# Fourier stage of a four-layer hybrid network: the order of the filler steps inside each slot

## The chip, the core and the metric

The kernel runs on one core of one Trainium2 chip, as one launch. The metric is the device time of a run in microseconds; the median of three runs of the kernel before is 4054.6 us.

## What is computed

The network has four layers on a tensor of 4 images, 96 channels and 64 x 64 pixels, all in float32: a state-space layer, a convolution block, an attention layer with a quantised feed-forward, and a Fourier mixing layer with another quantised feed-forward. The change touches the Fourier mixing alone. Its input is the token sequence `t` (4 batches of 4096 tokens of 96 channels), normalised over the channels:

```
def _ln_t(v, eps=1e-5):
    m = jnp.mean(v, axis=-1, keepdims=True)
    s = jnp.var(v, axis=-1, keepdims=True)
    return (v - m) / jnp.sqrt(s + eps)

h = jnp.einsum('bnc,hc->bnh', x, w1)
h = jax.nn.relu(_bn(h, bn1_gamma, bn1_beta, bn1_mean, bn1_var))
X = jnp.fft.fft(h, axis=1, norm='ortho')
rd = jnp.diagonal(r)
idg = jnp.diagonal(i)
xr = jax.nn.relu(X.real * rd - X.imag * idg + rb)
xi = jax.nn.relu(X.imag * rd + X.real * idg + ib)
y = jnp.fft.ifft(xr + 1j * xi, axis=1, norm='ortho').real.astype(jnp.float32)
o = jnp.einsum('bnh,ch->bnc', y, w2)
return _bn(o, bn2_gamma, bn2_beta, bn2_mean, bn2_var)

t = t + fourier(_ln_t(t))
```

The hidden width is 192, and the transform runs over the 4096 tokens.

## The kernel before

**Units and slots.** `fourier` (line 1083) cuts the work into 8 units, a unit being one batch and one half (96) of the hidden channels. A unit holds 24 groups of 4 channels and is worked on in 4 portions of 6 groups (`PER` = 4), so there are 32 portions, `its`. A loop over slots `j` (line 1259) is a software pipeline over them: slot j begins portion j and does later steps of earlier portions. The 4096-point transform is split into 128 x 32 points.

**The main steps of a slot**, in their order:

- `over_n1(j)` (line 1141): six products with `dft1` on PE (L1147) into `s1`, two multiplications by twiddle factors on DVE (L1151) into `p0` and `p1`, two additions on POOL (L1159) into `f`.
- `fold(j - 2)` (line 1189): a ReLU on ACT over half of `av` (L1193), four DVE operations (L1198, L1201) that add or subtract pairs into `zz` and `z64`, and a negation on ACT (L1204).
- `over_k1` of a first block (line 1233): part of the inverse transform of a unit two units back. It loads a table `gt` (L1235, on SP), runs four products (L1238), and copies the result to `ys` on ACT (L1240).
- `over_n2(j - 1)` (line 1161): four products with `dft2` (L1168 to L1171) into `xi` and `xr`, one DVE multiplication (L1174) into `ec`, twelve ACT operations (L1183) into `av`, and two additions on POOL (L1186, L1187).
- `w2` of the first block (line 1242, product L1246, addition to `t` on DVE at L1250 or L1252), then `over_k1` of a second block.
- `over_k2(j - 3)` (line 1206): twelve products (L1216, L1217) and two ACT copies to `bt` (L1218).
- `w2` of the second block.

Blocks of the inverse transform exist in slots 8 to 39, portions to begin in slots 0 to 31.

**The filler steps** prepare the next batch:

- `norm1` (line 1101) is the centring of 512 tokens: a product with a matrix of ones (L1104), the subtraction of the mean on DVE into `h` (L1105), the square on ACT into `ln_sq` (L1107). 
- `norm2` (line 1109) is the sum of squares of the same tokens: a product with ones (L1111), Ln and Exp on ACT into `ln_rs`, which has one buffer (L1113, L1114), and the multiplication of `h` on POOL (L1115). 
- `w1` (line 1126) is a token product: two products (L1133) and two ReLU evictions on ACT (L1135) into `hh`, for two of the 32 token columns at a time. It needs all of the batch's `h`.
- `row64` (line 1223) closes a unit's forward transform: a product (L1226), an ACT copy to `r64` (L1228), a DMA to DRAM (L1230) and a DMA from there into row 64 of `bt` (L1231). The first `over_k1` of that unit reads `bt`.

Slots 0 to 3, 8 to 11 and 16 to 19 hold norm steps (called norm slots here), 16 steps per batch; slots 4 to 7, 12 to 15 and 20 to 23 hold four token products each (token slots); `row64` falls in slots 7, 11, 15, 19, 23, 27, 31 and 35. Apart from row64, slots 24 to 31 have no filler.

**What sets the order.** The body runs under `tc.manual_schedule` for PE, DVE, ACT and POOL, so each of these engines issues its instructions in the order in which the Python code calls the steps. Before, the slot collects its main steps in a list `main` and its filler steps in a list `fill`, and spreads the filler evenly behind the main steps:

```
left = len(main)
for f0 in main:
    f0()
    take = -(-len(fill) // left)
    for f1 in fill[:take]:
        f1()
    fill, left = fill[take:], left - 1
```

SP, which issues the DMAs, is not in that set; its order comes from the scheduler.

**The ring of two banks.** `norm1`, `norm2`, `w1`, `row64`, `over_k1` and `w2` all take their result tile from `misc` (line 1097), a pool of two PSUM banks (`m_ps` in the profile). So each of these products waits until the product two before it in this ring has been read by its DVE or ACT reader. `s1`, `xi`, `xr` have one bank group each, `i1` two.

Of the kernel before, what the change touches and what calls it, by code (L numbers as in the profile page):

```python
# [18 lines left out]
B, C, HW, L = 4, 96, 64, 4096  # L19
# [3 lines left out]
MB = 512  # L23
# [27 lines left out]
class Net:  # L51
# [1031 lines left out]
    def fourier(self, dram, t, h):  # L1083
        tc, nc, ins = self.tc, self.nc, self.ins
        CG, G, K1 = 24, 6, 65
        PER = CG // G
        units = [(b, half) for b in range(B) for half in range(2)]
        its = [(u, g) for u in range(len(units)) for g in range(0, CG, G)]
        with ExitStack() as ctx:
# [11 lines left out]
            def norm1(b, a, kept):  # L1101
                ps = misc(C)
                x = t[:, b * L + a : b * L + a + MB]
                nc.tensor.matmul(ps, self.ones, x, start=True, stop=True)  # L1104
                nc.vector.scalar_tensor_tensor(h[:C, a : a + MB], ps, -1.0 / C, x, ALU.mult, ALU.add)  # L1105
                kept[a] = wk.tile([C, MB], F32, name="ln_sq", tag="sq", bufs=2)
                nc.scalar.activation(kept[a], h[:C, a : a + MB], AF.Square)  # L1107

            def norm2(a, kept):
                ps = misc(C)  # L1110
                nc.tensor.matmul(ps, self.ones, kept.pop(a), start=True, stop=True)  # L1111
                rs = wk.tile([C, MB], F32, name="ln_rs", tag="rs")
                nc.scalar.activation(rs, ps, AF.Ln, scale=1.0 / C, bias=self.eps[:C])  # L1113
                nc.scalar.activation(rs, rs, AF.Exp, scale=-0.5)  # L1114
                nc.gpsimd.tensor_mul(h[:C, a : a + MB], h[:C, a : a + MB], rs)  # L1115

            def norm(b):
                kept = {}
                steps = [lambda a=a: norm1(b, a, kept) for a in range(0, L, MB)]
                steps2 = [lambda a=a: norm2(a, kept) for a in range(0, L, MB)]  # L1120
                order = steps[:1]
                for one, two in zip(steps[1:], steps2):
                    order += [one, two]
                return order + steps2[-1:]

            def w1(b, n):

                if n == 0:
# [12 lines left out]
            def over_n1(i):  # L1141

                u, g = its[i]
                ps = pln.tile([128, 2, MB], F32, name="s1_ps", tag="s1")
                for d in range(G):
                    a = d % 3 * 2 * K1
                    nc.tensor.matmul(ps[:, d // 3, a : a + 2 * K1], hh[u][:, g + d], self.dft1, start=True, stop=True)  # L1147
                pp = []
                for k in range(2):
                    p = wk.tile([128, G, 2, K1], F32, name=f"p{k}", tag=f"p{k}")  # L1150
                    nc.vector.tensor_mul(  # L1151
                        p.rearrange("p (a g) r k -> p a g (r k)", a=2),
                        ps[:, :, : 6 * K1].rearrange("p a (g k) -> p a g k", g=3),
                        self.twid[:, k : k + 1, None, :].to_broadcast([128, 2, 3, 2 * K1]),
                    )
                    pp.append(p)
                f[i] = wk.tile([128, 2, G, K1], F32, name="f", tag="f", bufs=2)
                for r in range(2):
                    nc.gpsimd.tensor_add(f[i][:, r], pp[0][:, :, r, :], pp[1][:, :, 1 - r, :])  # L1159
# [29 lines left out]
            def fold(i):  # L1189

                u, g = its[i]
                v = av.pop(i)
                nc.scalar.activation(v[:, 1:3], v[:, 1:3], AF.Relu)  # L1193
                z = zz[i] = wk.tile([128, G, 3, K1 - 1], F32, name="zz", tag="zz", bufs=2)
                if g == 0:
                    z64[u] = wk.tile([128, 2, CG], F32, name="z64", tag="z64", bufs=2)
                for k, (one, two, op) in enumerate(((0, 2, ALU.add), (3, 1, ALU.subtract))):
                    nc.vector.scalar_tensor_tensor(  # L1198
                        z[:, :, 1 + k], v[:, one, :, : K1 - 1], 0.0, v[:, two, :, : K1 - 1], ALU.max, op
                    )  # L1200
                    nc.vector.scalar_tensor_tensor(  # L1201
                        z64[u][:, k, g : g + G], v[:, one, :, K1 - 1], 0.0, v[:, two, :, K1 - 1], ALU.max, op
                    )
                nc.scalar.mul(z[:, :, 0], z[:, :, 2], -1.0)  # L1204
# [18 lines left out]
            def row64(u):  # L1223
                ps = misc(CG)[:, :128]
                for k in range(2):
                    nc.tensor.matmul(ps, z64[u][:, k], self.dft64[:, k], start=k == 0, stop=k == 1)  # L1226
                r = wk.tile([CG, N2, 4], F32, name="r64", tag="r64", bufs=2)
                nc.scalar.copy(r, ps.rearrange("p (n c) -> p n c", c=4))  # L1228
                d = dram.tile([1, N2 * C], F32, name="d64", tag="d64", bufs=2)
                nc.sync.dma_start(d.rearrange("o (n g c) -> g (o n) c", n=N2, c=4), r)  # L1230
                nc.sync.dma_start(bt[u][64:65].rearrange("p n c -> p (n c)"), d)  # L1231

            def over_k1(u, n, kept):
                gt = wk.tile([N1, 4, N1], F32, name="gt", tag="gt", bufs=2)
                nc.sync.dma_start(gt, ins["idft"][:, n : n + 4])  # L1235
                ps = misc(C).rearrange("p (n a) -> p n a", n=4)
                for d in range(4):
                    nc.tensor.matmul(ps[:, d], bt[u][:, n + d], gt[:, d], start=True, stop=True)  # L1238
                kept[u, n] = wk.tile([C, MB], F32, name="ys", tag="ys", bufs=2)
                nc.scalar.copy(kept[u, n], ps.rearrange("p n a -> p (n a)"))  # L1240

            def w2(u, n, kept):

                b, half = units[u]
                ps = misc(C)
                nc.tensor.matmul(ps, self.a_w2[:, half, :], kept.pop((u, n)), start=True, stop=True)  # L1246
                ps = ps.rearrange("p (n a) -> p n a", n=4)
                td = ft[b][:, n : n + 4]
                if half == 0:
                    nc.vector.scalar_tensor_tensor(td, ps, self.b2, td, ALU.add, ALU.add)  # L1250
                else:
                    nc.vector.tensor_add(td, td, ps)  # L1252

            engines = {mybir.EngineType.PE, mybir.EngineType.DVE, mybir.EngineType.Activation, mybir.EngineType.Pool}
            with tc.manual_schedule(engines=engines):
                for n in range(0, N2, 2):
                    w1(0, n)
                kept = {}
                for j in range(len(its) + 12):
                    main, fill = [], []  # L1260
                    ub, k = divmod(j - 2 * PER, PER)
                    if j < len(its):
                        main.append(lambda j=j: over_n1(j))
                    blocks = [(ub, n) for n in (8 * k, 8 * k + 4)] if 0 <= ub < len(units) else []
                    if 2 <= j < len(its) + 2:
                        main.append(lambda j=j: fold(j - 2))
                    if blocks:
                        main.append(lambda: over_k1(*blocks[0], kept))
                    if 1 <= j < len(its) + 1:
                        main.append(lambda j=j: over_n2(j - 1))  # L1270
                    if blocks:
                        main.append(lambda: (w2(*blocks[0], kept), over_k1(*blocks[1], kept)))
                    if 3 <= j < len(its) + 3:
                        main.append(lambda j=j: over_k2(j - 3))
                    if blocks:
                        main.append(lambda: w2(*blocks[1], kept))

                    u, k = divmod(j, PER)
                    if (j - 7) % PER == 0 and 0 <= (j - 7) // PER < len(units):
                        fill.append(lambda j=j: row64((j - 7) // PER))  # L1280
                    if u + 2 < len(units):
                        b = u // 2 + 1
                        if u % 2 == 0:
                            steps = norm(b) if k == 0 else steps
                            fill += steps[4 * k : 4 * k + 4]
                        else:
                            fill += [lambda b=b, n=n: w1(b, n) for n in range(8 * k, 8 * k + 8, 2)]
                    left = len(main)
                    for f0 in main:
                        f0()  # L1290
                        take = -(-len(fill) // left)
                        for f1 in fill[:take]:
                            f1()
                        fill, left = fill[take:], left - 1


def build(tc, ins, out):
# [155 lines left out]
```

## Time and profile before

| What | us |
|---|---|
| runs: lowest, median, highest | 4048.9, 4054.6, 4059.6 |
| the profiled execution's own time | 4057.1 |
| its span, first to last instruction | 4054.9 |
| Fourier stage in the span, from the first token product to the next stage | 3316 to 3911 |
| slots 0 to 3, one by one | 7.8, 7.9, 9.1, 17.4 |
| slots 4 to 7, one by one | 20.8, 10.2, 10.4, 14.1 |
| slots 8 to 11, one by one | 20.4, 20.7, 20.6, 20.5 |
| slots 12 to 15, one by one | 18.7, 20.2, 20.2, 18.8 |
| slots 16 to 23 | as 8 to 15, within 0.3 |
| slots 24 to 31 | 11.6 each |

The length of a slot is the time from its first L1147 product to that of the next slot, read from the timeline of PE. Over the whole span PE is busy 82%, DVE 79%, POOL 73% and ACT 60%; most of it lies in other stages. The view of windows gives busy times for chosen stretches; the chain of waits follows the work that ended last backwards, so a line in it is something that delayed the end; in the timeline a bracket at the end of a line gives the idle time before it and what ended it.

### The profile page before, as it was taken

To read this page: it belongs to the slowest core of one execution; us is meant where nothing else is said; L and a number is where in the kernel's file an instruction comes from. 1 tells how busy PE (TensorE), PEld (TensorE's weight loads), DVE (VectorE), ACT (ScalarE), POOL (GpSimd) and SP (SyncE) were. 2 spreads that over 40 slices of the span, in tenths; PEclk is the share of its full clock that TensorE was granted. 3 is DMA by queue.
4 is the path that set the end of the run, shared out by engine and by line. 5 is a ranking of instruction groups with operands and counts; after the bars stand their busy time and mean duration, and the time that the engine had idled before them with its cause. 6 is when DMAs were issued, how large, how long until landed. Compare 5 with 4: busy or idle time off the path is not lost. (4 is left out here: it accounts for less than half of the span.)

```text
span 4054.9 us, 45522 instructions
## 1 busy us (share of the span) xinstructions
PE 3311.5 (82%) x14174; PEld 1426.9 (35%) x14174; DVE 3193.0 (79%) x2772; ACT 2423.0 (60%) x4644; POOL 2946.8 (73%) x1571
## 2 busy tenths in 40 slices
PE   6888888888888777888888887678999887887987
PEld 3222222222222222222222221376446345556642
DVE  5999999999999999999999999724632763443649
ACT  4666667666667666666766665322445665544547
POOL 2999999999999999999999999511010455333428
PEclk8788878888878888887888887668999998889989
DMA  7667567666756666675675666363000000001111
GB/s 182 144 158 172 136 150 169 158 148 163 175 130 167 168 148 160 158 171 135 162 173 141 160 165 159 103 189 136 0 1 1 1 6 3 27 27 30 45 43 54
DMA packets 183291, 468.13 MB, mean 115 GB/s; under 512 B 53236, under 2 KB 55166, under 8 KB 179968
## 3 DMA queue, kind: packets, MB, share of 16 engines
q1 hardware_dynamic: 183048, 465.21, 46.1%
q8 instruction: 113, 1.85, 0.2%
q14 instruction: 130, 1.06, 0.1%
HBM read 391.53 MB, written 73.50 MB: 115 GB/s over the span
## 5 line engine op out<-in xcount | busy, mean ns | idle before, releaser
L496 POOL TENSOR_TENSOR hs<-hs,crep 128x1024 f32<-128x1024 f32 x768 | 1797.1, 2363 | 28.8 <-DVE hs L490 24.0
L454 PE MATMUL rep<-dbl,sel_b 32*128 32x512 f32 x1152 | 403.8, 777 | 467.8 <-DVE hs L490 441.3
L474 POOL TENSOR_TENSOR up<-udb,brep 128x1024 f32<-128x1024 f32 x256 | 604.5, 2361 | 8.5 <-DMA brep<-cd 8.5
L468 ACT ACTIVATE da<-ddb,nega 128x1024 f32<-128x1024 f32 x512 | 584.8, 1149 | 13.5 <-DVE hs L490 6.9
L468 ACT ACTIVATE dap<-ddb,nega 128x1024 f32<-128x1024 f32 x256 | 286.3, 1118 | 419.9 <-DVE hs L490 417.9
L515 PE MATMUL y<-hs,sel_r 128*32 128x512 f32 x3072 | 477.9, 693 | 4.9 <-POOL hs L496 4.9
L490 DVE TENSOR_TENSOR_SCAN hs<-da,state,rep 128x1024 f32<-128x1024 f32 x192 | 450.9, 2348 | 16.7
L490 DVE TENSOR_TENSOR_SCAN hs<-da,state,u 128x1024 f32<-128x1024 f32 x192 | 450.9, 2348 | 11.2 <-DVE u L486 1.4
L490 DVE TENSOR_TENSOR_SCAN hs<-dap,state,up 128x1024 f32<-128x1024 f32 x192 | 447.2, 2329 | 6.4 <-ACT dap L468 6.0
L210 PE MATMUL ps<-n,w_x 97*64 97x512 f32 x1536 | 376.1, 633 | 6.9 <-ACT n L323 5.4
L454 PEld LDWEIGHTS rep<-dbl,sel_b 32*128 32x128 f32 x1152 | 108.4, 216 | 766.9 <-issue 519.3
L486 DVE TENSOR_TENSOR u<-udb,rep 128x1024 f32<-128x1024 f32 x256 | 314.7, 1229 | 46.2 <-PE rep L454 15.0
L486 DVE TENSOR_TENSOR rep<-udb,rep 128x1024 f32<-128x1024 f32 x256 | 310.8, 1214 | 0.3
L1038 POOL CAST hq<-y 128x512 fp8e5<-128x512 f16 x192 | 117.7, 638 | 222.3 <-issue 136.6
L210 PEld LDWEIGHTS ps<-n,w_x 97*64 97x64 f32 x1536 | 110.6, 143 | 261.5 <-issue 215.7
L1186 POOL TENSOR_TENSOR av<-av,ec 128x780 f32<-128x780 f32 x32 | 58.8, 1837 | 197.2 <-ACT av L1183 191.8
L515 PEld LDWEIGHTS y<-hs,sel_r 128*32 128x32 f32 x3072 | 65.7, 116 | 358.0 <-issue 190.0
L382 POOL TENSOR_TENSOR du<-delta,xc 128x512 f32<-128x512 f32 x96 | 122.8, 1279 | 66.0 <-DMA gp_x<-in_x 51.2
L224 PE MATMUL ps<-xc,xproj 64*102 64x512 f32 x384 | 160.9, 1001 | 3.5 <-ACT xc L344 3.5
L911 POOL MEMSET h<- 1x4096 f32 x1 | 3.5, 3506 | 212.4 <-DVE n L824 212.4
L358 ACT COPY dbl<-ps 102x512 f32<-102x512 f32 x64 | 34.4, 589 | 205.7 <-PE ps L224 205.7
L490 DVE TENSOR_TENSOR_SCAN hs<-da,rep 128x1024 f32<-128x1024 f32 x64 | 146.5, 2289 | 5.4
(256 smaller groups left out, 6573.1 us busy)
## 6 DMA issues: line engine op xcount, KB each, us to landing
ddb<-dd SPq DMA_DIRECT2D x768, 128.0 KB, 3.6
udb<-ud SPq DMA_DIRECT2D x768, 128.0 KB, 4.4
crep<-cd SPq DMA_DIRECT2D x512, 128.0 KB, 4.3
brep<-cd SPq DMA_DIRECT2D x256, 128.0 KB, 3.4
dd<-delta SPq DMA_DIRECT2D x64, 384.0 KB, 4.9
ud<-du SPq DMA_DIRECT2D x192, 128.0 KB, 2.4
band<-in_band SPq DMA_DIRECT2D x24, 1024.0 KB, 5.8
gt<-in_idft SPq DMA_DIRECT2D x64, 256.0 KB, 2.8
```

What stands on the lines that cost most here:

```text
L210: nc.tensor.matmul(ps[rows], w[:, 64 * p : 64 * p + 64], rhs[:, at.start + shift : at.stop + shift], start=k == 0, stop=k == len(ws) - 1, ...
L224: nc.tensor.matmul(ps, w[rows, p], x[rows, p], start=start and p == 0, stop=p == 2)
L382: nc.gpsimd.tensor_mul(u, m["delta"][:, of], m["xc"][:, of])
L454: nc.tensor.matmul(x[:, at], sel_b[rows, order[t][1]], made[k]["dbl"][rows, at], start=True, stop=True)
L468: nc.scalar.activation(da, made[k]["dd", h, j], AF.Exp, scale=nega[:, col : col + 1])
L474: nc.gpsimd.tensor_mul(u, made[k]["ud", h, j], made[k]["brep", g])
L486: nc.vector.tensor_mul(u, made[k]["ud", h, j], x)
L490: nc.vector.tensor_tensor_scan(hs[:, 1:], made[k].pop(("da", t)), u, 0.0 if s == 0 else st, ALU.mult, ALU.add)
L496: nc.gpsimd.tensor_mul(hs[:, :T], hs[:, 1:], made[k]["crep", order[t][1]])
L515: nc.tensor.matmul(made[k]["y", p][row : row + 32], sel_r, made[k]["hs", t][:, at], start=False, stop=True, skip_group_check=True,)
L1038: nc.gpsimd.tensor_copy(q[:, m, :], y2, saturate=False)
L1186: nc.gpsimd.tensor_add(v[:, 2:4], v[:, 0:2], ec)
```

## The change

The even spreading is gone. The function `norm`, which made the list of norm steps, is removed, and the loop calls each step in an order written out by hand. The steps, their instructions, their tiles and buffers, and the slot in which each main step stands are the same. In a norm slot k = 0 to 3 of a batch, `norm1` of block 2k comes before the fold, `norm2` of the block before it after the first `over_k1`, `norm1` of block 2k + 1 after `over_n2`, and `norm2` of block 2k after `over_k2`; the last `norm2` of the batch ends slot k = 3. In a token slot, two token products come before the fold and two after `over_k2`; in the first token slot (k = 0) the first two come after the second `over_k1` instead. `row64`, which before came directly after `over_n1`, comes after `over_k2`, ahead of the last token products and the last `w2`.

```
-            def norm(b):
...
-                return order + steps2[-1:]
...
-                kept = {}
+                kept, sq = {}, {}
                 for j in range(len(its) + 12):
...
+                    def turn(count):
+                        for _ in range(min(count, len(tokens))):
+                            w1(b, tokens.pop(0))
+
                     if j < len(its):
+                        over_n1(j)
+
+                    if normed:
+                        norm1(b, a, sq)
+                    if k:
+                        turn(2)
                     if 2 <= j < len(its) + 2:
+                        fold(j - 2)
                     if blocks:
+                        over_k1(*blocks[0], kept)
+                    if normed and k:
+                        norm2(a - MB, sq)
                     if 1 <= j < len(its) + 1:
+                        over_n2(j - 1)
+                    if normed:
+                        norm1(b, a + MB, sq)
                     if blocks:
+                        w2(*blocks[0], kept)
+                        over_k1(*blocks[1], kept)
+                    if not k:
+                        turn(2)
                     if 3 <= j < len(its) + 3:
+                        over_k2(j - 3)
+                    if normed:
+                        norm2(a, sq)
+                    if (j - 7) % PER == 0 and 0 <= (j - 7) // PER < len(units):
+                        row64((j - 7) // PER)
+                    turn(len(tokens))
                     if blocks:
+                        w2(*blocks[1], kept)
+                    if normed and k == PER - 1:
+                        norm2(a + MB, sq)
```

Here `a` is the first token of block 2k, `b` the next batch, `normed` is true in the norm slots, and `tokens` holds the four token products of a token slot.

## The prediction on record

> **What bounds the kernel now.** The change lies in the Fourier stage, 3316 to 3911 us, so the page's 79 to 82% shares, ruled by layer 0, say little. I read the windows of that stage first. The rows shown are cut where the kind of filler changes, by the start of each slot's first over_n1 product: slots 0 to 7 (norm, then tokens, without the inverse transform), 8 to 11 (norm), 12 to 15 (tokens), 24 to 31 (no filler). 16 to 23 repeat 8 to 15. Columns: window, length, busy time and instructions of PE, PEld, DVE, ACT and POOL, clock, DMA.
>
> ```profile
> core 0: us, PE busy (x) PEld busy (x) DVE busy (x) ACT busy (x) POOL busy (x), PEclk, DMA share, GB/s
> 3333.45:3431.14 97.69, 78.10 (x372) 57.87 (x373) 37.60 (x55) 59.03 (x164) 48.68 (x37) 0.91 0.01 1
> 3431.14:3513.39 82.25, 67.80 (x292) 42.33 (x293) 34.72 (x43) 40.05 (x94) 34.32 (x25) 0.86 0.09 27
> 3513.39:3594.00 80.61, 64.08 (x341) 50.48 (x339) 31.26 (x38) 37.85 (x109) 24.59 (x17) 0.96 0.10 27
> 3751.79:3844.42 92.63, 84.26 (x522) 63.64 (x521) 61.82 (x72) 53.72 (x146) 47.07 (x31) 1.00 0.17 47
> ```
>
> Four norm slots take 82.2 us and four token slots 80.6, while eight slots without filler take 92.6, or 11.6 each. Filler costs 9 us a slot, though its PE work is 4 products of 0.86 = 3.4 us (norm) or 8 of 0.46 = 3.7 us (tokens), from start to start in the timeline. In the norm slots the clock is 0.86. No engine is full: the stage runs on waits. The chain of waits between 3450 and 3480 us shows one whole period.
>
> ```profile
> 3453.03 0.87 PE m_ps L1111 x2
> ...
> 3454.70 0.63 ACT ln_rs L1114
> 3455.34 0.75 ACT av L1193
> ...
> 3457.31 1.22 DVE z L1201
> 3458.53 0.47 DVE zz L1198
> 3459.00 0.08 DVE z L1201
> 3459.08 0.61 DVE h L1105
> 3459.69 0.04 issue
> 3459.73 2.02 PE m_ps L1111 x2
> 3461.75 1.30 PE xi_ps L1168 x2
> ```
>
> A sum of squares (L1111) heads the slot; its Ln and Exp hold ACT until 3455.3; only then comes the fold's ReLU (L1193), then the fold on DVE, then the subtraction (L1105) that frees one of the two m banks, and only then may PE run the next sum of squares and, behind it in order, over_n2. PE idles 3.89 us there and then runs slowly. The waits of PE on the token side have the same shape:
>
> ```profile
> 3535.29 1.04 PE L1238 MATMUL m_ps<-gt,bt 128*96 128x128 f32 x8
> 3539.44 1.35 PE L1133 MATMUL m_ps<-a_w,h 97*128 97x192 f32 x4 [3.11 <-ACT hh L1135]
> ```
>
> The second token product's eviction stands behind the fold's negation on ACT, and the fourth user of the bank waits for it.
>
> **What the skill says.** The Trainium skill, TensorE: Matmul & The Clock Gate, Part 1: idle time drops the array to half its clock for about a window of activity. The trace agrees: xi_ps takes 1.30 to its successor after the 3.89 us wait, 0.65 in a plain slot, where gaps of 1.2 us leave the clock at 1.00. Same page, Architectural detail: ACT, DVE and POOL are strict first-in-first-out; agrees, since ready evictions wait behind the fold. SBUF — State Buffer, Two separate sides: a DVE operation with two SBUF inputs and a GpSimd one exclude each other; agrees: the fold's four operations take 2.9 us beside L1159 and 1.1 us alone. DMA: Bandwidth & Descriptors, Rules for kernel authors: issue a DMA early and wait late; the change does the opposite for row64, costed below.
>
> **Part by part.** No instruction is added or removed; the order of the two built programs does differ as the diff says on PE, DVE, ACT, POOL and SP. Times t count from the slot's first over_n1 product. I walk each engine's new order by hand with durations of the trace.
>
> *Norm slot with blocks (9, 10, 17, 18).* PE: over_n1 to 1.34, centring product to 2.2. DVE: twiddles 1.6 to 3.4, subtraction to 4.05. PE: over_k1 to 3.15, waits 0.95 for the subtraction's bank, sum of squares 4.1 to 4.95, over_n2 (4 x 0.65) to 7.6. ACT: square to 4.65, ReLU to 5.5; the fold no longer meets L1159 (3.5 to 5.35), so 1.1 us, to 6.6; negation 7.1, ys 7.6, Ln and Exp 8.75, twelve av to 12.3. PE: second centring waits for ys's bank to 7.7, ends 8.55; w2 9.4; over_k1 10.35; over_k2 (2.68) 13.0; sum of squares 13.9; w2 14.75. ACT then has square, ys, two bt, Ln and Exp and ends at 15.4, before the next square at 18.8. POOL has the first multiply by ln_rs (L1115, 1.26) at 8.85 to 10.1, the av pair to 16.1 and the second multiply to 17.35, before the next ReLU (19.4) and twiddle sum (18.2); ln_rs has one buffer, so each Ln waits for the multiply before it, 10.1 here and 14.2 when it is wanted. Now 20.7, then 14.75: **-6.0 x 4 = -23.8**. The new wait, ReLU behind the square, costs the ReLU about 1 us against now, and is paid for by the missing Ln and Exp. Slots 8 and 16 lack one sum of squares (13.85), but meet row64 (below): 20.5 to 14.3, **-12.3** for two. Slots 11 and 19 have a third sum of squares, row64 and waits of w2 and of that sum for their banks; its Ln waits for POOL's av pair and multiply and runs 2 us into the next slot, hidden by that slot's row64 wait: 20.5 to 16.5, **-8**.
>
> *Token slot (13, 14, 21, 22).* PE: over_n1 1.34, two token products 3.15, over_k1 4.1 (its bank's evictions are first on ACT, 2.9), over_n2 6.7. ACT: evictions to 3.75, ReLU 4.55; fold beside L1159 until 5.4, to 6.5; negation, ys 7.35; av to 10.9. w2 waits for ys, 7.5 to 8.4; over_k1 9.3; over_k2 12.0; two token products 13.8; w2 14.65. Now 20.2: **-5.55 x 4 = -22.2**. Slots 15 and 23 add row64 and a token product that waits for its copy: 18.8 to 15.7, **-6.2**.
>
> *Slots 0 to 7.* Same walk: slots 0 to 3 41.4 against 42.2 (POOL's av pair, 3.7, and two Ln/Exp pairs still end slot 3); slot 4 14.0 against 20.8, since over_n2 now covers most of the 8.82 us that the first token product waits for POOL; 5 and 6 stay at 10.3; slot 7 12.6 against 14.1. **-9**.
>
> *row64, moved from the slot's head to its end.* Its copy starts two DMAs on SP that the next unit's first over_k1 needs.
>
> ```profile
> 3876.40 0.33 SPq L1230 DMA_DIRECT2D d<-r x1
> 3878.02 0.33 SPq L1235 DMA_DIRECT2D gt<-in_idft x1
> 3880.51 0.24 SPq L1231 DMA_DIRECT2D bt<-d x1
> ```
>
> Issue to issue is 2.9 to 4.4 us over the eight, and PE starts 2.1 us after the last second issue (3882.61): 5.1 to 6.5 us from copy to product. Now over 10 us of work covers it (3788.6 to 3799.4 in slot 27) except once, at the tail. SP is in order, but in the new program the next unit's first two gt loads stand ahead of d, and the eight behind bt aren't due for a slot, so no load is late. Cover left after the copy: row64's followers plus over_n1, 4.35 (slots 8, 16), 2.3 (12, 20), 3.7 (24), 1.85 (28), 0.45 (32). The uncovered rest, less 1.2 us that w2's wait for ys gives back, with 5.8 for the pair: slots 8, 16 inside the numbers above; 12, 20: 3.5 - 1.1 = +2.4, which with a clean walk of 16.4 (the first two token products there wait for w2's addition to 8.4 and for the second ys to 10.15) makes 18.8 against 18.75, **0**; 24 +1, 28 +2.7, 32 +4.1, tail (36, later by w2 and over_k1) +2: **+9.8**. A PE wait of that length lets the clock drop; after 2.2 to 3.9 us it cost 1.75 to 2.75 us in the norm slots (row of L1111 to w2, 6.1 and 7.1 against 4.34 warm); 2 x 4 boundaries (12, 20, 28, 32) = **+8**.
>
> *Sum.* -23.8 - 12.3 - 8 - 22.2 - 6.2 - 9 + 9.8 + 8 = -63.7. The profiled execution took 4057.1 (span 4054.9 and 2.2 around it), so 3993.4; it lies 2.5 above the median 4054.6 of the three, so **3991**. Unknown ends: fold beside POOL 1.1 or 2.9 (8 norm slots: 0 to +14); DMA pair 5.1 to 6.5 (-5 to +5); clock drops at none or all eight boundaries (-8 to +14); handshakes of the walk, -0.2 to +0.5 a slot over 16 (-3 to +8).
>
> **Rivals.** *Row chain hidden.* If fold and ACT catch up during the wait, the +9.8 + 8 and the two +2.4 vanish: 3991 - 23 = 3968. For: DVE and ACT are 42 to 49% busy there. Against: plain slots have only 1.2 us of PE idle. *New order binds elsewhere.* The square ahead of the ReLU makes the fold the chain again, 1.8 us in eight norm slots, and the clock drops once in each of 16 slots (1.0 on average): -64 becomes -34, 4021. For: ReLU is the start of every chain today. Against: the walk leaves it 3 us. *Slower.* The row chain dominates: place, the eight unit boundaries; the clean gain is 64 + 9.8 + 8 + 4.8 = 87 us, so it turns when a boundary costs over 87/8 = 10.9 us, and ends at 4071 at 13 us each (10 us of wait and 3 of cold clock). For: SP is in order and holds bt until d has landed. Against: the pair is 6.5 at most today. *No change*: order arrives but the waits move whole, 4055; the plain slots, 11.6 on the same queues, speak against it.
>
> **Numbers.** Forecast 0.58, hidden 0.16, binds elsewhere 0.17, no change 0.05, slower 0.04. 0.3% (12 us) is about what a measurement of this kernel can tell. Faster 0.91, same 0.05, slower 0.04. Range 3960 to 4022: it takes in the hidden case, the one that binds elsewhere and most of the sum of the unknown ends, and leaves the last two out.
>
> **What would show it.** Right: norm slots of 14.5 to 15.5 us and token slots near 15; L1105 no longer releasing L1111 for 3.89 us; clock above 0.93 between slots 8 and 23; the first over_k1 of a unit waiting on a DMA for 1 to 5 us. Wrong: slots still near 20 with another releaser of PE, or DMA waits over 8 us at each boundary.

## The result and the profile after

The changed kernel took 4006.5 us (median of four runs, 4002.6 to 4009.9) against 4054.1 for the kernel before beside it: ratio 0.9876, 95% interval 0.9864 to 0.9888. In a later measurement beside the kernel before (run after_again below) it was 4003.6 against 4053.0, ratio 0.9877, 0.9861 to 0.9892. The forecast was 3991, the range 3960 to 4022.

Two profiled executions of the changed kernel are used, one of 4009.9 us ("after") and one of 4000.7 ("after_again"). From the first token product to the next stage's first product the Fourier stage took 597.1 us before, 544.5 in the first and 537.1 in the second: 52.6 and 60.0 less. Code lines below over_n1 are 9 lower than before (over_n1 is L1138, `over_k1` L1229).

The windows of the profile after, cut like those of before: slots 0 to 7, 8 to 11, 12 to 15 and 24 to 31.

```profile
core 0: us, PE busy (x) PEld busy (x) DVE busy (x) ACT busy (x) POOL busy (x), PEclk, DMA share, GB/s
3335.96:3431.80 95.84, 80.79 (x373) 59.31 (x373) 40.70 (x55) 59.12 (x164) 50.38 (x38) 0.92 0.01 1
3431.80:3493.90 62.10, 59.25 (x293) 38.67 (x294) 30.05 (x44) 39.82 (x96) 31.28 (x24) 0.96 0.11 35
3493.90:3561.00 67.10, 60.26 (x325) 49.32 (x324) 27.93 (x36) 36.95 (x107) 24.99 (x18) 0.95 0.12 33
3687.82:3792.79 104.97, 85.77 (x522) 64.95 (x520) 64.36 (x77) 55.45 (x148) 48.94 (x32) 0.98 0.15 41
```

Four norm slots went from 82.2 to 62.1 us and four token slots from 78.0 (3513.39 to 3591.35; the window shown with the prediction reached 2.6 us into slot 16) to 67.1; PE is busy nearly all of a norm slot now, and the granted clock (PEclk) rose from 0.86 to 0.96. Slots 0 to 7 hardly moved (97.7 to 95.8), and the eight slots without filler became **longer**, 92.6 to 105.0 (slot 31 here runs to the first `over_k1` of slot 32, so that product's wait is in it). The chain of waits after shows slot 9, the period that headed the prediction:

```profile
3447.45 1.35 PE s_ps L1138 x12
3448.88 1.84 DVE p L1142 x2
3450.73 0.61 DVE h L1105
3451.38 1.10 PE m_ps L1111 x2
3452.48 0.66 PE xi_ps L1159 x2
...
3455.10 0.95 PE m_ps L1104 x2
3456.05 0.86 PE m_ps L1237 x2
3456.91 1.03 PE m_ps L1229 x8
...
3460.62 0.86 PE m_ps L1111 x2
3461.49 0.86 PE m_ps L1237 x2
3462.34 1.35 PE s_ps L1138 x12
```

The fold, its ReLU and Ln and Exp are gone from the chain. The subtraction (L1105) stands right behind the twiddles; from there on PE runs from product to product, `xi_ps` at 0.66 instead of 1.30. The waits of PE in the stage show what went and what came (columns: total, times, longest). Before:

```profile
PE m_ps L1111 <- DVE h L1105: 20.8, 7, 3.9
```

After:

```profile
PE m_ps L1229 <- DMA bt<-d: 16.6, 5, 5.6
...
PE m_ps L1229 <- issue: 8.3, 2, 4.8
PE m_ps L1111 <- DVE h L1105: 6.9, 7, 1.8
```

L1105 held PE for 20.8 us before and holds it for 6.9 now, at most 1.8. New are waits of a unit's first `over_k1` for row 64; the two put down to "issue" are of the same kind. The start of slot 12, on PE and on SP:

```profile
3498.73 1.99 PE L1229 MATMUL m_ps<-gt,bt 128*96 128x128 f32 x8 [3.33 <-DMA bt<-d]
3500.51 1.49 PE L1159 MATMUL xi_ps<-f,dft 128*128 128x390 f32 x2
```

```profile
3492.88 0.33 SPq L1221 DMA_DIRECT2D d<-r  x1
3496.05 0.24 SPq L1222 DMA_DIRECT2D bt<-d  x1
```

Row64's copy ends near 3492.9, the second DMA is issued 3.2 us later, and PE gets its data another 2.7 us later: 5.9 us, of which PE's other work covers 2.5. The eight products then take 1.99 us instead of 1.04.

### The profile page after: what moved, and what is told of

It is laid out like the page before. It is cut to its first block, busy times and chain, and to the rows that moved or that the text cites. A ratio compares the mean times of both kernels' runs of the same rounds, so it can differ in the third digit from the quotient of the medians.

```text
span 4007.8 us, 45514 instructions
## 1 busy us (share of the span) xinstructions
PE 3303.4 (82%) x14174; PEld 1425.1 (36%) x14174; DVE 3186.9 (80%) x2772; ACT 2421.0 (60%) x4644; POOL 2944.4 (73%) x1571
## 5 line engine op out<-in xcount | busy, mean ns | idle before, releaser
L468 ACT ACTIVATE da<-ddb,nega 128x1024 f32<-128x1024 f32 x512 | 584.9, 1149 | 14.9 <-DMA ddb<-dd 7.4
L210 PE MATMUL ps<-n,w_x 97*64 97x512 f32 x1536 | 368.0, 622 | 8.1 <-ACT n L323 5.4
L486 DVE TENSOR_TENSOR u<-udb,rep 128x1024 f32<-128x1024 f32 x256 | 314.6, 1229 | 42.1 <-PE rep L454 10.9
```

Of the source, the lines that this page charges most:

```text
L210: nc.tensor.matmul(ps[rows], w[:, 64 * p : 64 * p + 64], rhs[:, at.start + shift : at.stop + shift], start=k == 0, stop=k == len(ws) - 1, ...
L468: nc.scalar.activation(da, made[k]["dd", h, j], AF.Exp, scale=nega[:, col : col + 1])
L486: nc.vector.tensor_mul(u, made[k]["ud", h, j], x)
```

## The experiments

The theory: the new order of norm and token steps gives the gain; the late row64 gives part of it back through its two DMAs and the slow products after them. The rivals are in the expectations. Each run was timed against the kernel before on the same chip.

### Row64 at the head; row64 without its DMAs

a_row_head moves the call in the changed kernel:

```
 over_n1(j)
+if (j - 7) % PER == 0 and 0 <= (j - 7) // PER < len(units):
+    row64((j - 7) // PER)
...
-if (j - 7) % PER == 0 and 0 <= (j - 7) // PER < len(units):
-    row64((j - 7) // PER)
```

> The changed kernel with row64 called directly behind over_n1 again, as in the kernel before; everything else as changed. Theory (the late row64 leaves its pair of DMAs uncovered at the start of the next unit, and PE idles there and then runs slowly): about 25 us less than the changed kernel, so near 3981 us; slots 12 and 20 from 22.2 and 21.0 to about 16.6 us, slot 28 from 15.8 to 11.6, slots 32 and 33 together 9 less, no wait of PE for bt<-d; slots 11 and 19 may grow by up to 1 us. Rival (the wait for row64 is slack that was displaced; moved away, the same engines wait elsewhere): within 5 us of the changed kernel, 4001 to 4011 us, with slots 12 and 20 still above 20 us under another releaser. Rival (place in the ring of two banks): row64 at the head costs slots 11, 15, 19, 23 what it saves in the next ones, so also near 4006.

a_no_row_dma leaves it late and drops its DMAs, so that row 64 of the inverse transform's input is left out:

```
-d = dram.tile([1, N2 * C], F32, name="d64", tag="d64", bufs=2)
-nc.sync.dma_start(d.rearrange("o (n g c) -> g (o n) c", n=N2, c=4), r)
-nc.sync.dma_start(bt[u][64:65].rearrange("p n c -> p (n c)"), d)
```

> The changed kernel without the two DMAs of row64 (its product and copy stay at their new place); row 64 of the inverse transform's input is thus left out. Theory (the DMA pair is what is late): as with row64 at the head, 3978 to 3986 us, no DMA wait ahead of the first over_k1 of a unit. Rival (row64's product and copy, at their late place in the ring of two banks and on ACT, are what costs): near 4006 us, slots 12 and 20 still above 20.

Measured: 3974.7 us (ratio 0.9798, 0.9785 to 0.9810) and 3973.9 (0.9795, 0.9782 to 0.9807). Both lie some 32 us below the changed kernel, where 25 and 20 to 28 had been expected, and within 1 us of each other. **The DMAs are nearly all of the cost.** Row64's late place in the ring and on ACT shows in a_no_row_dma too, but only as 0.6 to 0.9 us in each of slots 11, 15, 19, 23, 27 and 31 against a_row_head. The wait is no displaced slack. Where the 34.5 us of the stage went, after less a_row_head: slots 12 and 20 6.0, slot 28 4.2, slots 32 and 33 with the wait at the head of 32 8.6, from slot 34 to the end of the stage 7.3, the rest 8.4 in small pieces. One wait for row 64 is left in a_row_head, 1.00 us at slot 36. Slots 12 and 20 stayed at 18.6 and 18.5, not 16.6. The PE timeline of a_row_head in slot 12 tells why:

```profile
3493.51 0.82 PE L1162 MATMUL xr_ps<-f,dft 128*128 128x390 f32 x2
3497.39 1.81 PE L1237 MATMUL m_ps<-ys,a_w2s 96*96 96x512 f32 x2 [3.06 <-ACT ys L1231]
```

And ACT at the same time:

```profile
3490.84 0.68 ACT L1113 ACTIVATE ln_rs<-m_ps,eps 96x512 f32<-96x512 f32 x1 [1.84 <-PE s_ps L1138]
3491.55 0.63 ACT L1114 ACTIVATE ln_rs<-ln_rs 96x512 f32<-96x512 f32 x1
3492.09 0.84 ACT L1184 ACTIVATE av<-av 128x780 f32<-128x780 f32 x1
```

The batch's last Ln and Exp stand ahead of the fold's ReLU (L1184). (The line names PE as releaser of that Ln; the multiplication on POOL that frees the one `ln_rs` ended at the same time.) The fold, its negation and `ys` behind it are late, and `w2` waits 3.06 us. The prediction had this step, "hidden by that slot's row64 wait"; take the row64 wait away, and it shows. The order on ACT alone does not set the price, though. In slot 12 of a_no_row_dma the same Ln and Exp stand ahead of the ReLU, but the Ln starts 0.64 us into the slot instead of 1.51, and `w2` waits 1.22 us (both lines from that run):

```profile
3496.34 0.68 ACT L1113 ACTIVATE ln_rs<-m_ps,eps 96x512 f32<-96x512 f32 x1 [1.68 <-POOL h L1115]
3501.92 1.10 PE L1234 MATMUL m_ps<-ys,a_w2s 96*96 96x512 f32 x2 [1.22 <-ACT ys L1228]
```

Slot 20 has the same two times there and took 16.6 us; slot 12 took 18.2, as later products of it ran slowly.

### Row64 late in the kernel before

```
-fill.append(lambda j=j: row64((j - 7) // PER))
+main.insert(len(main) - bool(blocks), lambda j=j: row64((j - 7) // PER))
```

> The kernel before with row64 alone at the changed place (behind over_k2, ahead of the last w2); all other filler spread as before. Theory: slower than the kernel before by 12 to 20 us: slot 28 by about 4 and slots 32 and 33 by about 9, as in the changed kernel, and slots 12 and 20 by 0 to 4 each, since those slots still wait elsewhere. Rival (displaced slack): within 4 us of the kernel before, because the wait only takes the place of others; then the cost in the changed kernel would come only from the new order around it.

Measured: 4076.4 us against 4058.4, ratio 1.0044 (1.0032 to 1.0056), 18 us more; the stage grew from 597.1 to 614.9. Slots 24 and 28 grew by 3.8 and 3.9, slots 12 and 20 by 1.3 each, the wait at the head of slot 32 made 6.1, and 11, 15, 19 and 23 grew by 2.0 to 2.2, while slot 16 shrank by 3.3. In 11, 15, 19 and 23 the edit also moves the other filler up one place, as row64 no longer stands ahead of it in `fill`; what of their growth is row64's is not shown. In all, the late row64 costs about the same under the old order.

### Each order alone

Both start from the kernel before, with the token products or the norm steps called in the changed kernel's order and the other filler spread evenly; row64 stays. The cores of the edits:

```
+if not first:
+    turn(2)
 if 2 <= j < len(its) + 2:
     main.append(lambda j=j: fold(j - 2))
...
+if first:
+    turn(2)
 if 3 <= j < len(its) + 3:
     main.append(lambda j=j: over_k2(j - 3))
+turn(len(todo))
```

> The kernel before with the token products alone in the new order (two ahead of the fold, two behind over_k2); row64 behind over_n1, norm steps spread as before. Theory (each kind of filler waits on its own slots): slots 13, 14, 21, 22 at 14.7 us instead of 20.2, slots 15 and 23 at about 16 instead of 18.8, slots 12 and 20 at 16.6 to 18 instead of 18.7, slot 4 some 5 us shorter: 32 to 40 us less than before, 4014 to 4022. Rival (one order alone keeps the clock up, or waits pass from the token slots into the norm slots behind them): less than 20 us less, or more than 50.

```
+put(True, norm1, b, a, sq)
 if 2 <= j < len(its) + 2:
     main.append(lambda j=j: fold(j - 2))
...
+put(kn, norm2, a - MB, sq)
 if 1 <= j < len(its) + 1:
     main.append(lambda j=j: over_n2(j - 1))
+put(True, norm1, b, a + MB, sq)
```

> The kernel before with the norm steps alone in the new order; token products spread as before, row64 behind over_n1. Theory (gains of the two orders add): the changed kernel with row64 at the head is 84 us below before and the token order alone 38, so the norm order gives 46: 4008 to 4016 us, slots 9, 10, 17, 18 at 14.9 instead of 20.7, slots 13 and 14 still at 20.2. Rival (one order enables the other, as through the clock): less than 35 or more than 57 us below before.

Measured: tokens alone 4020.5 us (ratio 0.9909, 0.9896 to 0.9922), 37.9 below before, as expected in all, though slot 4 became 1.3 us shorter, not 5, and slot 8 became 1.4 shorter; norm alone 4021.9 (0.9915, 0.9902 to 0.9929), with slots 9, 10, 17 and 18 at 14.9 as expected, 36.5 below, less than the 46 expected, though not as little as the rival's 35. The expectation had compared with a_row_head, which is not quite "row64 as before": slot 35 has no over_n1, and there the even spreading had put row64 **behind** the first `over_k1`. Against the run that restores even that (a_tail_k1, below, ratio 0.9818), the gains add: 0.91% + 0.85% = 1.76%, against 1.82% (1.67 to 1.98). Neither order needs the other.

### Which part of the norm order

In a_sq_first (from a_row_head) the two norm steps around the fold change places:

```
-if normed:
+if normed and k:
+    norm2(a - MB, sq)
+elif normed:
     norm1(b, a, sq)
...
 if normed and k:
-    norm2(a - MB, sq)
+    norm1(b, a, sq)
```

> The changed kernel with row64 directly behind over_n1, and in each norm slot but a batch's first the two norm steps around the fold exchanged: the sum of squares of the block before ahead of the fold, the centring behind the first over_k1. Two accounts of why the norm slots took 20.7 us before. Account 1 (Ln and Exp ahead of the fold's ReLU on ACT delay the chain that over_n2 waits for): slots 9, 10, 11, 17, 18, 19 grow by 2 to 3 us each, 12 to 18 in all, 3987 to 3993 us. Account 2 (the subtraction L1105 behind the fold holds a bank that a ring step ahead of over_n2 needs; Ln and Exp as such cost nothing): here no ring step stands between that centring and over_n2, so less than 1 us a slot, 3972 to 3981 us.

Measured: 3979.6 us (ratio 0.9812, 0.9797 to 0.9826); slots 9, 10, 17 and 18 at 15.4 instead of 14.9, slots 11 and 19 at 16.6 instead of 16.0: account 2. Slot 9 of a_sq_first on PE:

```profile
3447.34 1.10 PE L1104 MATMUL m_ps<-t,ones 96*96 96x512 f32 x2
3448.28 0.82 PE L1159 MATMUL xi_ps<-f,dft 128*128 128x390 f32 x2
...
3450.25 0.82 PE L1162 MATMUL xr_ps<-f,dft 128*128 128x390 f32 x2
3452.35 1.10 PE L1104 MATMUL m_ps<-t,ones 96*96 96x512 f32 x2 [1.29 <-DVE h L1105]
```

Ln and Exp run ahead of the ReLU, the fold is late and slow (its first two DVE operations take 1.20 and 1.22 us), and L1105 behind it starts only at 3451.6. But `over_n2` no longer stands behind a step that needs the bank, so PE works meanwhile and waits 1.29 us. By this run the old order cost so much because a ring step whose bank was held behind the fold stood **ahead of over_n2**; the length of the ACT queue by itself was worth 0.6 us.

### The length of a wait, tried in the tail

From slot 36 on, PE only alternates `over_k1` and `w2`. Two kernels move the row64 of slot 35 alone: a_tail_head from the changed kernel, where the other seven stay late, and a_tail_k1 from a_row_head, where this one goes behind the first `over_k1`.

```
+if j == len(its) + PER - 1:
+    row64(len(units) - 1)
...
-if (j - 7) % PER == 0 and 0 <= (j - 7) // PER < len(units):
+if (j - 7) % PER == 0 and 0 <= (j - 7) // PER < len(units) and j < len(its):
     row64((j - 7) // PER)
```

```
-if (j - 7) % PER == 0 and 0 <= (j - 7) // PER < len(units):
+if (j - 7) % PER == 0 and 0 <= (j - 7) // PER < len(units) and j < len(its):
     row64((j - 7) // PER)
...
 over_k1(*blocks[0], kept)
+if (j - 7) % PER == 0 and len(its) <= j < 4 * len(units) + 7:
+    row64((j - 7) // PER)
```

> The changed kernel once more, on the same chip as the three runs below, to compare them with: 4002 to 4010 us.

> The changed kernel with the last row64 alone (slot 35) at the head of its slot, ahead of the first over_k1; the other seven stay late. Theory (the length of a wait decides whether the array stays at full speed: 1.0 us at the tail keeps blocks at 2.70, 2.8 us and more puts the next five at 4.45): the tail goes from 45.2 to about 38 us, 7 us less than the changed kernel. Rival (only the wait itself counts, 4.8 us against 1.0): 3 to 4 us less.

> The changed kernel with row64 directly behind over_n1, and in slot 35, which has no over_n1, behind the first over_k1, the true place of the kernel before. Theory (same threshold): the wait for bt<-d grows from 1.0 to about 2.8 us and the next blocks run at 4.45: the tail is 45 to 47 us instead of 37.9, 7 to 9 us more than with row64 at the head everywhere, 3982 to 3984. Rival (only the wait counts): 2 us more.

Measured: the changed kernel 4003.6 us, a_tail_head 3994.5 (ratio 0.9853, 0.9839 to 0.9867), a_tail_k1 3980.4 (0.9818, 0.9802 to 0.9833). The tail, here from the first `over_k1` of slot 34 to the next stage, took 44.7 us in after_again, 37.6 in a_tail_head (7.1 less), 46.2 in a_tail_k1 and 37.9 in a_row_head (8.3 apart), 46.6 before. The PE timeline of a_tail_head at the wait:

```profile
3825.84 1.09 PE L1229 MATMUL m_ps<-gt,bt 128*96 128x128 f32 x8 [0.78 <-DMA bt<-d]
3827.64 1.10 PE L1237 MATMUL m_ps<-ys,a_w2s 96*96 96x512 f32 x2 [0.72 <-ACT ys L1231]
3828.58 1.04 PE L1229 MATMUL m_ps<-gt,bt 128*96 128x128 f32 x8
```

And that of a_tail_k1:

```profile
3802.32 1.99 PE L1229 MATMUL m_ps<-gt,bt 128*96 128x128 f32 x8 [2.39 <-issue]
3805.04 2.02 PE L1237 MATMUL m_ps<-ys,a_w2s 96*96 96x512 f32 x2 [0.72 <-ACT ys L1231]
3806.85 1.91 PE L1229 MATMUL m_ps<-gt,bt 128*96 128x128 f32 x8
...
3820.21 1.83 PE L1229 MATMUL m_ps<-gt,bt 128*96 128x128 f32 x8
3822.77 1.10 PE L1237 MATMUL m_ps<-ys,a_w2s 96*96 96x512 f32 x2 [0.73 <-ACT ys L1231]
3823.71 1.04 PE L1229 MATMUL m_ps<-gt,bt 128*96 128x128 f32 x8
```

The wait before was 2.80 us:

```profile
3882.61 1.99 PE L1238 MATMUL m_ps<-gt,bt 128*96 128x128 f32 x8 [2.80 <-issue]
```

Waits of 0.78 and 1.00 us (a_row_head) leave the step from block to block at 2.70 us; 2.39 here and 2.80 before are followed by four steps near 4.5 and one of 3.5, 4.83 after by two near 4.5 and one of 3.5. A wait 1.4 us longer (2.39 against 1.00) cost 8.3 us. The rival, that only the wait counts, is out; that a longer wait (4.83) was followed by fewer slow blocks was not foreseen.

A sharp threshold is not shown either. Two runs of this document that keep row64 at the head wait 1.18 us (a_sq_first) and 1.82 (a_last_norm, described below) at the same place. Their first products run at full speed, and later ones slow down. a_sq_first, then a_last_norm:

```profile
3807.71 1.08 PE L1229 MATMUL m_ps<-gt,bt 128*96 128x128 f32 x8 [1.18 <-DMA bt<-d]
...
3810.71 1.91 PE L1229 MATMUL m_ps<-gt,bt 128*96 128x128 f32 x8
```

```profile
3800.78 1.08 PE L1229 MATMUL m_ps<-gt,bt 128*96 128x128 f32 x8 [1.82 <-DMA bt<-d]
...
3804.08 1.92 PE L1229 MATMUL m_ps<-gt,bt 128*96 128x128 f32 x8
```

Their tails took 40.8 and 40.0 us, between the 37.9 and the 46.2 above.

### Towards a better kernel

a_last_norm (from a_row_head) moves a batch's last sum of squares, a_row_early adds row64 a slot earlier, a_best adds late token products in slots 4, 12 and 20.

```
+if b < B and not normed and not k and u > 1:
+    norm2(L - MB, sq)
 if 1 <= j < len(its) + 1:
     over_n2(j - 1)
...
-if normed and k == PER - 1:
+if normed and k == PER - 1 and not u:
     norm2(a + MB, sq)
```

> The changed kernel with row64 directly behind over_n1, and a batch's last sum of squares moved from the end of slots 11 and 19 behind the first over_k1 of slots 12 and 20. Theory (its Ln waits for POOL, runs into the next slot ahead of the fold's ReLU, and w2 there waits 3.1 us for ys; the late row64 had hidden this): slots 12 and 20 from 18.6 and 18.5 to about 16.6, slots 11 and 19 from 16.0 to about 15, 4 to 6 us less than with row64 at the head alone (3974.7). Rival (the wait comes back at the first token product, which needs that block's multiplication on POOL): within 2 us of 3974.7.

```
-if (j - 7) % PER == 0 and 0 <= (j - 7) // PER < len(units):
-    row64((j - 7) // PER)
+if (j - 6) % PER == 0 and 0 <= (j - 6) // PER < len(units):
+    row64((j - 6) // PER)
```

> As the run with the last sum of squares moved, and row64 one slot earlier than in the kernel before, directly behind over_n1 of slots 6, 10, 14 and so on. Theory: the only wait for bt<-d that is left with row64 at the head, 1.0 us in the tail, goes; 1 to 2 us less. Rival (a copy on ACT and a ring step more in slots 10, 14, 18, 22 cost more than in 11, 15, 19, 23): 1 to 3 us more.

```
-if not k:
-    turn(2)
```

> As the run with row64 one slot earlier, and in the first token slots (4, 12, 20) all four token products behind over_k2. Theory (slots 12 and 20, 19.4 and 20.5 us there, stand on two short waits of the first token products, for POOL and for ys, and on the slow array after them): both slots at 15 to 16.6 us, 6 to 10 us less: 3961 to 3965. Rival (four token products in a row on two banks wait for their evictions behind bt's copies): within 2 us of 3970.9.

Measured: 3972.9 us (ratio 0.9793, 0.9780 to 0.9806), 3970.9 (0.9791, 0.9777 to 0.9804) and 3965.4 (0.9782, 0.9767 to 0.9796). The first two can't be told from a_row_head. In a_last_norm slots 11 and 19 fell from 16.0 to 14.9 as expected, but slot 12 rose to 20.5 and slot 20 fell only to 17.9: the first two token products waited 0.63 us for POOL and 1.43 for `ys`, after which the products ran slowly in slot 12. The rival was right. In a_row_early the tail's wait went (tail 35.5 us), but slots 12 and 20 took 19.4 and 20.5. With the token products late, the windows of a_best for slots 8 to 11 and 12 to 15 read:

```profile
3432.81:3491.46 58.65, 55.87 (x290) 36.70 (x291) 29.30 (x43) 39.16 (x95) 30.61 (x24) 1.00 0.12 37
3491.46:3551.04 59.58, 57.80 (x328) 46.74 (x326) 27.74 (x36) 37.41 (x109) 26.48 (x19) 1.00 0.12 36
```

Both are at full clock, and slots 12 and 20 take 15.5 us. Slot 4 grew from 15.4 to 17.0, and the gain over a_row_early was 5.5 us instead of the 6 to 10 expected. a_best runs 38 us below the changed kernel and 88 below the one before, on one chip.

## Why the prediction was right, step by step

Slot lengths from the two profiled executions, against the kernel before:

| Term | predicted | after | after_again |
|---|---|---|---|
| norm slots 9, 10, 17, 18 | -23.8 | -23.2 | -23.2 |
| slots 8, 16 | -12.3 | -10.9 | -11.7 |
| slots 11, 19 | -8 | -7.4 | -7.4 |
| token slots 13, 14, 21, 22 | -22.2 | -22.0 | -22.0 |
| slots 15, 23 | -6.2 | -6.8 | -6.8 |
| slots 0 to 7 | -9 | -1.9 | -3.3 |
| slots 12, 20 (0, clock +4) | +4 | +5.6 | +3.4 |
| slots 24 to 27 | +1 | +1.7 | +1.0 |
| slots 28 to 33 (2.7 + 4.1, clock +4) | +10.8 | +13.7 | +12.1 |
| tail, from slot 34 | +2 | -1.4 | -1.9 |
| sum | -63.7 | -52.6 | -59.8 |

**The walk by hand** held: slot 9 ends L1105 at 4.05 us and starts its sum of squares at 4.10 where the walk has 4.05 and 4.1, and the steady norm and token slots came within 0.25 us of it. The diff does what it says, the wait for L1105 is cut to 1.8, the clock between slots 8 and 23 is 0.95 to 1.00, and the units' first `over_k1` waits 1.5 to 5.6 us for DMAs (0.9 to 5.1 in after_again), except in slot 8. For the old norm slot the prediction named the whole chain from Ln and Exp to `over_n2`; a_sq_first shows which link counts, as Ln and Exp ahead of the fold cost little without the ring step ahead of `over_n2`. The prediction also puts the slow fold of before down to L1159 alone; in its own lines the second slow operation (L1201, 1.22 us from 3457.31) comes after L1159 has ended at 3456.97, beside the multiplication L1115 on POOL.

**Row64** was priced at 9.8 + 8 + 4.8 = 22.6 us (the rival that ends slower names the sum). After_again less a_tail_k1, whose row64 is where the kernel before has it, is 23.2 us in the medians and 19.1 in the stage. That is more than the rival "hidden" allows and far below the 87 at which the change would have turned. Its distribution was off: slots 28 to 33 cost 1 to 3 more, the tail 3 to 4 less, since the kernel before already had the 2.80 us wait there and with it the five slow blocks. That the sum came so close, while its parts did not, is in part luck.

**The clean gain** was put too high: 87 us, where a_tail_k1 lies 72.6 below before (79.1 in the stage). Two terms were mis-sized. Slots 0 to 7, "-9": the walk gave slots 0 to 3 41.4 us; they took 44.5, longer than the 42.2 before, as sums of squares there wait up to 3.2 us for the Ln of one two steps before (L1113); and row64 adds 1.0 to 1.3 to slot 7. Slots 12 and 20, "a clean walk of 16.4": 18.7 and 18.5 in a_tail_k1, where the last Ln and Exp run ahead of the fold's ReLU as late as in a_row_head. The walk had this step in slots 11 and 19, but not its price once nothing covered it. Where the Ln comes earlier the walk is right: b_tokens has 16.6 in both slots.

**The rest.** Of the 15 us between 3991 and the median, 4 to 11 are in these terms. In both executions the last stage took 2.9 to 3.0 us longer than before (141.4). Over all the runs it lay between 137.0 and 144.5; no run ties that to the change, and its cause stays open. The two executions of the same kernel differ by 7 us in the stage, in part in how long products stayed slow (slot 12 22.2 or 20.6).

## What to carry to other kernels

Where a ring of few banks is shared by steps of several engines, put the step whose reader queues behind a long chain ahead of that chain, and put no step that needs its bank ahead of work that needs none. When filler is reordered, place every step that starts a transfer by its consumer's time, not by what is convenient on the computing engines: one `row64` call, moved by 9 to 14 us in most of its slots, cost 23 us of a gain of 73. Count a wait of PE with the slow products after it; in the tail here, where PE idles between products anyway, they cost 7.9 us after a wait of 2.39, 4.4 after 4.83 and none after 1.00.

## What was not expected of the hardware

- The length of a single wait of PE does not decide whether slow products follow. In the tail, 1.00 us left the `over_k1` products at 1.04 to 1.08 us, 1.18 slowed later ones, and 2.39 doubled the next ones at once. Where PE has fewer gaps, waits of 1.2 us in six of the slots 24 to 31 before and of 2.22 at the head of slot 24 after were followed by no slow product.
- Slow products can come after short waits too. In slot 12 of the changed kernel the products are slow for about 3 us after the wait of 3.33 (3498.7 to 3501.8), then at full speed, and slow again from 3508.2 to 3512.0 after waits of 0.47 and 0.81. In slot 12 of after_again nearly the same waits (0.45 and 0.83) are followed by L1207 at 0.39 us. The lines of the changed kernel:

```profile
3502.50 0.82 PE L1161 MATMUL xr_ps<-f,dft 128*128 128x390 f32 x2
...
3508.16 1.50 PE L1124 MATMUL m_ps<-a_w,h 97*128 97x192 f32 x4 [0.81 <-ACT ys L1231]
3509.45 0.64 PE L1207 MATMUL i_ps<-dft,zz 128*128 128x128 f32 x2
```

- How long products stay slow differs more than the wait does. In the tail it was about 21 us after 2.39 us (3802.3 to 3823.7 in a_tail_k1) and about 12 after 4.83 (3836.0 to 3848.5 in the changed kernel). What sets this stays open.
